# The third channel mix's down product by two levels, with its sums of quarters in fewer operations

## The chip, the cores and the metric

The kernel runs on one core of a Trainium2 chip. The metric is the device time of one execution in microseconds (us), the median of several runs. Engines are named as the profile names them: PE is the matrix engine (PEld its weight loads), DVE the vector engine, ACT the scalar engine, POOL the engine whose queue issues the weight sums' transfers here, SP the engine whose queue issues most loads.

## The reference

The input is x, 2048 tokens of 512 channels, float32. All products are in float32.

```python
n = layernorm(x)
h = layernorm(n) * ln1_g + ln1_b;  hh = h shifted by one token
k, v, r = (h*m + hh*(1-m)) @ W.T            # three mixes m, three weights 512 x 512
n = n + sigmoid(r) * wkv(k, v) @ Wo.T
h = layernorm(n) * ln2_g + ln2_b;  hh = h shifted by one token
kk = (h*cm_mk + hh*(1-cm_mk)) @ Wkey.T      # 512 -> 2048
kv = silu(kk) @ Wval.T                      # 2048 -> 512: the channel mix's down product
sr = sigmoid((h*cm_mr + hh*(1-cm_mr)) @ Wcr.T)
x = x + n + sr * kv
z = layernorm(x)
out = x + (silu(z @ Wg.T) * (z @ Wu.T)) @ Wd.T   # 512 -> 2048 -> 512
```

## The kernel before, in words

**Tiling.** The 2048 tokens are four blocks of 512. A product of 512 tokens with a 512 x 512 weight is a "unit". Tokens, inputs and outputs are halved, and most units use a fast 2 x 2 scheme with seven products instead of eight (`unit`; only six early units go plainly, `plain_unit`). Each of the seven is a product of 256 x 256 x 256: four matmuls of 128 x 128 by 256 columns. Three of the seven use sums of the weight's quarters (S1, S2, S3, S4 stand for the four sums), and operands use T1 to T4, sums of the activation's quarters. T3 is written over the quarter B12.

**Weight sums.** `prepare` is a generator for one weight: four loads of 256 KB on POOL's queue, four additions or subtractions on DVE (128 x 512 each), each followed by a store of 256 KB to scratch memory in DRAM. `prepare_all` queues them, and `prep_one` advances the first one by one operation when a credit (`credit`, raised by a fixed amount per tick) allows it. Products fetch weights through a ring of 12 tiles of 256 KB on SP's queue (`ring`).

**Parts.** The first part goes through the time mix (k, r, v and output units) and the channel mix of each block: a gate unit, four key units (`up_unit`, whose results pass through silu on ACT), and the down product (`down_unit`). Blocks overlap: the next block's mixes and norms are made on DVE and ACT while PE works on this block. The last part (`ffn_gate`, `ffn_up`, `ffn_down`) takes the four blocks one after the other.

**Down products.** In the channel mix, `down_unit` is one unit over four groups of 512 inputs: each of the seven products adds up over four groups, 28 group products of four matmuls. In the last part, `down_product` applies the scheme twice: the seven outer products (listed in `DOWN`, as A11 x B11, S4 x B22, S2 x T2, A12 x B21, S1 x T1, S3 x T3, A22 x T4, called steps here) are each split again in seven inner products, so there are 49. An inner product has four matmuls of 128 x 128 by 128 columns, one per group, and one weight load of 256 KB. Inside a step (`steps`) the inner products come in the order A11 B11, A12 B21, S2 T2, S4 B22, S1 T1, S3 T3, A22 T4; the last two are held back (`held`) and put between the first products of the next step. `quarter_sums` makes the inner sums (T1, T2, T4, T3 of quarters) of a step's operand on DVE in four operations of 128 x 512; it is asked for after the last inner product of the step two before. The sums lie in two sets of four tiles, used in turn (`room["sets"]`); seven of these eight tiles are one of the three large operand tiles (`op_tile`), taken when the last part begins. `summed` adds a step's result r into the outer results and hands finished ones to `sink`.

**Order.** PE, DVE and ACT execute exactly in the order in which the program issues to them (`manual_schedule`). A planner in the program decides that order: `tick` is called once per product, adds the product's planned length to a slack, and issues DVE work as long as the slack is positive: first the `hot` list (urgent sums), else prepared weights by credit, else the `background` list (norms, mixes). If a product needs an operand whose sums are not issued yet, `run_one(True)` issues them at that point, directly ahead of the product. `need(name)` does the same for a whole background job. `later(fn, n)` postpones a function by n products. A mix (`mix`) needs a free operand tile before it starts: at most three live at a time.

Of the kernel before, what the change touches and what calls it, by code (L numbers as in the profile page):

```python
# [9 lines left out]
F32 = mybir.dt.float32  # L10
# [5 lines left out]
P = 128  # L16
# [16 lines left out]
WK, WV, WR, WO, WCR = range(5)  # L33

TURNED = 2
PLAIN = {(0, WK), (0, WR), (0, WV), (0, WO), (1, WK), (1, WR)}
# [25 lines left out]
def rwkv_ffn_kernel(  # L62
# [4 lines left out]
    vecs: bass.AP,  # L67
    w: bass.AP,
    wd: bass.AP,
    out: bass.AP,  # L70
# [11 lines left out]
    up = ctx.enter_context(tc.tile_pool(name="up", bufs=6))  # L82
    small = ctx.enter_context(tc.tile_pool(name="small", bufs=3))
    ps = ctx.enter_context(tc.tile_pool(name="ps", bufs=6, space=bass.MemoryType.PSUM))
    pv = ctx.enter_context(tc.tile_pool(name="pv", bufs=1, space=bass.MemoryType.PSUM))
# [5 lines left out]
    htp = mixes.enter_context(tc.tile_pool(name="htp", bufs=2))  # L91
    prep = mixes.enter_context(tc.tile_pool(name="prep", bufs=6))
    pools = {"q": mixes.enter_context(tc.tile_pool(name="qp", bufs=30))}

# [27 lines left out]
    for n in range(NW):  # L122
        sources[n], sums[n] = parts(n), scratch(f"sum{n}", 4)
    for k in range(4):
        sources["d", k] = [wd[q, k] for q in range(4)]
        sums["d", k] = scratch(f"d{k}", 4)
    for q in (A11, A12, A22, S1, S2, S3, S4):
        sources["dd", q] = [wd[q, k] if q < 4 else sums["d", k][q - 4] for k in range(4)]
        sums["dd", q] = scratch(f"dd{q}", 4)

# [15 lines left out]
    def prepare(n, own):  # L146

        raw = []
        for k in range(4):
            t = prep.tile([P, 2, HB], F32, tag="raw", name="raw") if own else q_tile("q")  # L150
            paced(nc.gpsimd.dma_start(flat(t), sources[n][k]))
            raw.append(t)
        yield 1
        a11, a12, a22, a21 = raw
        for k, o, i0, i1, op in (
            (0, a22, a21, a22, ALU.add),
            (2, a21, a11, a21, ALU.subtract),
            (1, a11, a22, a11, ALU.subtract),
            (3, a12, a12, a11, ALU.subtract),
        ):  # L160
            tt(o, i0, i1, op)
            nc.gpsimd.dma_start(sums[n][k], flat(o))
            yield

    def ring(src):
        t = wring.tile([P, 2, HB], F32, tag="w", name="w")
        nc.sync.dma_start(flat(t), src)
        return t
# [6 lines left out]

    def down_weight(q, k):

        if k >= 4:
            need_sums(("dd", q))
            src = sums["dd", q][k - 4]  # L180
        elif q >= 4:
            need_sums(("d", k))
            src = sums["d", k][q - 4]
        else:
            src = wd[q, k]
        return ring(src).rearrange("p a (h c) -> p (a h) c", c=P)
# [62 lines left out]
    credit = [0.0, 0.0]  # L249

    def prep_one():
        item = preps[0]
        if item[1] > 0:
            return False
        try:
            if next(item[2]) is not None:
                item[1] = WAIT
        except StopIteration:
            preps.popleft()
            finished.add(("sums", item[0]))  # L260
            if len(preps) > 1 and item[3] > 1:
                begin(preps[1])
            elif preps:
                begin(preps[0])
        return True

# [6 lines left out]
    def prepare_all(ns, own, depth):  # L273
        empty = not preps
        for n in ns:
            preps.append([n, 0, prepare(n, own), depth, False])
        if empty:
            for item in list(preps)[:depth]:
                begin(item)
# [731 lines left out]
    def up_unit(b, g):  # L1011
# [3 lines left out]
        def sink(i, j, c):  # L1015
            t = q_tile("s")
            nc.scalar.activation(t, c, AF.Silu)
            s[i, j] = B[(B11, B12, B21, B22)[2 * i + j]] = t

# [11 lines left out]
    def down_unit(b):  # L1031
# [8 lines left out]

        unit([WVAL + g for g in range(4)], [Lazy((b, g)) for g in range(4)], sink, True, done)

# [53 lines left out]
    def ffn_up(b, g):  # L1096
        s = gated.pop((b, g))
        hid = hidden.setdefault(b, {})

        def sink(i, j, c):  # L1100
            q = (B11, B12, B21, B22)[2 * i + j]
            if q not in hid:
                hid[q] = hidden_tile()
            tt(hid[q][:, g], c, s[i, j], ALU.mult)
            if g == 3:
                made.add((b, q))
                if q in (B11, B22):
                    quarter_sums(b, 0 if q == B11 else 1)

        def done():  # L1110
            if g == 0:
                for t in (T1, T2, T4):
                    hid[t] = hidden_tile()
            urgent((b, "f", g), sums_of({t: hid[t][:, g] for t in hid}))
            if g == 3:
                made.update((b, t) for t in (T1, T2, T4, "T3"))

# [4 lines left out]

    hidden, made, asked = {}, set(), set()
    room = {}
# [5 lines left out]
    def last_room():  # L1130

        room["hidden"] = ctx.enter_context(tc.tile_pool(name="hidden", bufs=7))
        pools["q"] = ctx.enter_context(tc.tile_pool(name="fq", bufs=15))
        more = ctx.enter_context(tc.tile_pool(name="more", bufs=1))
        m, _ = op_tile("quads")
        tiles = [m[:, k] for k in range(7)]
        tiles.append(more.tile([P, 2, HB], F32, name="quad"))
        tiles = [t.rearrange("p a (h c) -> p (a h) c", c=P) for t in tiles]
        room["sets"] = tiles[:4], tiles[4:]

    def quarters(t):
        return {2 * k + m: t[:, :, k, m * P : (m + 1) * P] for k in range(2) for m in range(2)}

    def quarter_operand(b, n):

        x = quarters(hidden[b][DOWN[n][1]])
        new = room["sets"][n % 2]
        x[T1], x[T2], x[T4] = new[:3]
        x["T3"] = new[3] if n < 2 else x[B12]
        return x  # L1150

    def quarter_sums(b, n):
        x = quarter_operand(b, n)
        asked.add((b, n))

        def run():
            for o, i0, i1 in (T1, B12, B11), (T2, B22, T1), (T4, B21, T2), ("T3", B22, B12):
                tt(x[o], x[i0], x[i1], ALU.subtract)
                yield

        urgent((b, "quarters", n), run())

    def down_product(b, sink, final):
        base = {}

        def summed(n, r):
# [26 lines left out]
            else:  # L1193
                add("u2", "u2")
                sink(1, 0, base["u2"])

        def steps(n):
# [3 lines left out]
            st = {}  # L1201
            x = quarter_operand(b, n)

            def product(dst, q, k, first):
                if k in (T1, T2, T4, "T3"):
                    while (b, n) not in asked:
                        flush_one()
                    while (b, "quarters", n) not in finished:
                        run_one(True)
                wt = down_weight(a, q)  # L1210
                for g in range(4):
                    mm = nc.tensor.matmul(  # L1212
                        dst,
                        lhsT=x[k][:, g, :],
                        rhs=wt[:, g, :],
# [41 lines left out]
            def seventh():  # L1257
# [9 lines left out]
                if n + 2 < 7:  # L1267
                    quarter_sums(b, n + 2)
                summed(n, r)

# [3 lines left out]
        for n in range(7):  # L1274
            t = DOWN[n][1]
            while (b, t if t != T3 else "T3") not in made:
                flush_one()
            one = steps(n)
# [21 lines left out]
    def ffn_down(b):  # L1300
# [18 lines left out]

        down_product(b, sink, final)  # L1320

    early = [WV, WCR, WO] + [WKEY + g for g in range(4)] + [WVAL, WVAL + 1]
    late = [n + g for g in range(4) for n in (WG, WU)] + [("dd", A11)]
    late += [("d", k) for k in range(4)] + [("dd", q) for q in (S4, S2, A12, S1, S3, A22)]

# [27 lines left out]
    for b in range(NB):  # L1355
# [6 lines left out]
        if b + 1 < NB:  # L1362
            out_unit(b + 1)
        need((b, "ck"))
        if nxt:
            push(f"norm{b + 2}", time_norm(b + 2))
        for g in range(4):
            up_unit(b, g)
            if b == 1 and g == 0:
                credit[1] = 0.55  # L1370
            if g == 0:
# [11 lines left out]
        if b == NB - 1:  # L1383
            push((0, "z", "t"), ffn_in(0), op_free)
        down_unit(b)
        if nxt:
            for n, u in (("k", k_unit), ("r", r_unit), ("v", v_unit)):
                u(b + 2)
    while preps:
        need_sums(preps[-1][0])  # L1390
    need((0, "z"))
    ffn_gate(0, 0)
    mixes.close()
    last_room()
    for b in range(NB):
        for g in range(4):
# [16 lines left out]
def _layout(inputs):  # L1413
# [32 lines left out]
    )  # L1446
    def quarter_quarter(i, j, m, k):
        at = slice(i * HB + m * P, i * HB + (m + 1) * P)
        lo = j * HB + k * P

        q = [down[at, g * H + lo : g * H + lo + P].T for g in range(4)]
        return np.stack(q, axis=1).reshape(P, 4 * P)

    places = ((0, 0), (0, 1), (1, 1), (1, 0))
    wd = np.stack(
        [np.stack([quarter_quarter(i, j, m, k) for m, k in places]) for i, j in places]
    )
# [3 lines left out]
        "vecs": np.ascontiguousarray(vecs),  # L1461
        "w": np.ascontiguousarray(w),
        "wd": np.ascontiguousarray(wd),
    }
# [19 lines left out]
```

## Time and profile before

| | |
|---|---|
| Median of 3 runs | 1238.17 us (1238.16 to 1238.85) |
| Profiled execution | 1239.38 us, of it the span from first to last instruction 1237.6 us |
| PE busy | 1228.9 us, 99% of the span |
| PE's weight loads | 1101.8 us, 89% |
| DVE busy | 711.9 us, 58% |
| ACT busy | 358.0 us, 29% |
| POOL busy | 153.1 us, 12% |
| DMA | 293.27 MB, mean 237 GB/s |
| Mean granted PE clock | 0.998 |

The third block's channel mix (blocks are counted from 0 in the code, so it is block 2) has its down product at about 506 to 562 us, overlapped at both ends with the last key unit and the fourth block's gate unit. The last part runs from about 645 us to the end; its first down product is at 770 to 818 us.

In a row of the timeline, the first figure is the start, the second the time that the merged instructions took, then engine, line, operation, output and input tiles, and the number of instructions; what stands in brackets is idle time of that engine before the row and what ended it. Each float32 matmul has two records.

### The profile page before, as it was taken

To read this page: it belongs to the slowest core of one execution; us is meant where nothing else is said; L and a number is where in the kernel's file an instruction comes from. 1 tells how busy PE (TensorE), PEld (TensorE's weight loads), DVE (VectorE), ACT (ScalarE), POOL (GpSimd) and SP (SyncE) were. 2 spreads that over 40 slices of the span, in tenths; PEclk is the share of its full clock that TensorE was granted. 3 is DMA by queue.
4 is the path that set the end of the run, shared out by engine and by line. 5 is a ranking of instruction groups with operands and counts; after the bars stand their busy time and mean duration, and the time that the engine had idled before them with its cause. 6 is when DMAs were issued, how large, how long until landed. Compare 5 with 4: busy or idle time off the path is not lost.

```text
span 1237.6 us, 18092 instructions
## 1 busy us (share of the span) xinstructions
PE 1228.9 (99%) x6524; PEld 1101.8 (89%) x6524; DVE 711.9 (58%) x1315; ACT 358.0 (29%) x663; POOL 153.1 (12%) x278
## 2 busy tenths in 40 slices
PE   8999999999999999999999999999999999999998
PEld 7888888888888888888888888998899888998898
DVE  5877686587684757533542365556546365563466
ACT  5534352252532425202311222212221222112211
POOL 1332221222212121222100000000000000000000
PEclk9999999999999999999999999999999999999999
DMA  5768995889877887898756645895459755785576
GB/s 184 255 216 281 311 314 199 307 310 316 276 245 246 291 273 241 261 319 301 248 143 191 215 144 157 270 334 154 143 182 310 271 145 149 239 300 156 153 217 209
DMA packets 139871, 293.27 MB, mean 237 GB/s; under 512 B 17528, under 2 KB 18696, under 8 KB 138504
## 3 DMA queue, kind: packets, MB, share of 16 engines
q1 hardware_dynamic: 116736, 219.20, 56.2%
q0 software_dynamic: 21440, 70.27, 15.5%
q10 hardware_dynamic: 1608, 2.65, 0.6%
q8 instruction: 53, 0.87, 0.3%
q14 instruction: 34, 0.28, 0.1%
HBM read 250.11 MB, written 41.95 MB: 236 GB/s over the span
## 4 chain that ended last, share of the span: by engine, by line
PE 96%; DVE 2%; ACT 1%; DMA 1%; issue 0%; DVEq 0%
PE ps L558 54%; PE ps L1212 14%; PE accv L558 11%; PE accx L558 11%; PE ps L660 5%; PE ps L443 1%; DVE e L395 0%; DMA w<-in_w 0%; DVE mix L395 0%; DMA x<-in_x 0%; ACT mix L873 0%; ACT hT_a L865 0%; DVE q L387 0%; ACT mix L496 0%; DVE st L401 0%; DVE resid L387 0%
## 5 line engine op out<-in xcount | busy, mean ns | idle before, releaser
L558 PE MATMUL ps<-zT,w 128*128 128x256 f32 x1280 | 289.5, 379 | 0.0
L558 PEld LDWEIGHTS ps<-zT,w 128*128 128x128 f32 x1280 | 241.9, 190 | 32.2
L558 PE MATMUL ps<-mix,w 128*128 128x256 f32 x920 | 210.7, 379 | 0.0
L558 PEld LDWEIGHTS ps<-mix,w 128*128 128x128 f32 x920 | 174.5, 190 | 23.6
L387 DVE TENSOR_TENSOR u<-u,accx 128x512 f32<-128x512 f32 x66 | 45.2, 686 | 115.5 <-ACT accx L593 115.5
L1212 PE MATMUL ps<-w,hid 128*128 128x128 f32 x832 | 104.5, 275 | 0.0
L558 PE MATMUL ps<-w,t 128*128 128x256 f32 x456 | 102.2, 379 | 0.0
L1212 PEld LDWEIGHTS ps<-w,hid 128*128 128x128 f32 x832 | 99.8, 192 | 0.8
L558 PEld LDWEIGHTS ps<-w,t 128*128 128x128 f32 x456 | 86.4, 190 | 11.7
L1212 PE MATMUL ps<-w,quads 128*128 128x128 f32 x704 | 89.0, 275 | 0.4 <-ACT r L1224 0.4
L578 ACT COPY accv<-ps 128x512 f32<-128x512 f32 x66 | 37.7, 570 | 176.5 <-PE ps L558 175.4
L1212 PEld LDWEIGHTS ps<-w,quads 128*128 128x128 f32 x704 | 84.2, 192 | 0.9 <-ACT r L1224 0.5
L593 ACT COPY accx<-ps 128x512 f32<-128x512 f32 x66 | 37.7, 571 | 153.7 <-PE ps L558 152.0
L387 DVE TENSOR_TENSOR u<-ps,u 128x512 f32<-128x512 f32 x66 | 45.6, 691 | 62.6 <-PE ps L558 62.2
L387 DVE TENSOR_TENSOR raw<-raw 128x512 f32<-128x512 f32 x92 | 63.3, 688 | 20.1 <-DMA raw<-d 10.7
L589 ACT COPY u<-ps 128x512 f32<-128x512 f32 x66 | 38.6, 585 | 122.9 <-PE ps L558 122.9
L660 PE MATMUL ps<-mix,w 128*128 128x256 f32 x320 | 72.4, 386 | 1.1 <-DVE mix L395 1.1
L1224 ACT COPY r<-ps 128x128 f32<-128x128 f32 x112 | 29.8, 266 | 142.1 <-PE ps L1212 142.1
L660 PEld LDWEIGHTS ps<-mix,w 128*128 128x128 f32 x320 | 61.4, 194 | 10.2 <-DVE mix L395 1.8
L1306 POOL DMA_DIRECT2D out<-resid x12 | 8.6, 716 | 491.5 <-DVE resid L387 491.5
L558 PE MATMUL accv<-zT,w 128*128 128x256 f32 x256 | 60.6, 379 | 0.0
L558 PE MATMUL accx<-zT,w 128*128 128x256 f32 x256 | 60.5, 379 | 0.0
(168 smaller groups left out, 1654.4 us busy)
## 6 DMA issues: line engine op xcount, KB each, us to landing
w<-sum SPq DMA_DIRECT2D x312, 256.0 KB, 3.4
w<-in_w SPq DMA_DIRECT2D x254, 256.0 KB, 3.8
w<-dd SPq DMA_DIRECT2D x112, 256.0 KB, 3.6
raw<-in_w POOLq DMA_DIRECT2D x48, 256.0 KB, 5.5
sum<-raw POOLq DMA_DIRECT2D x48, 256.0 KB, 4.2
w<-d SPq DMA_DIRECT2D x48, 256.0 KB, 3.7
q<-in_w POOLq DMA_DIRECT2D x36, 256.0 KB, 6.3
sum<-q POOLq DMA_DIRECT2D x36, 256.0 KB, 4.7
```

The costliest lines, as they stand in the source:

```text
L387: nc.vector.tensor_tensor(out, a, b, op)
L443: nc.tensor.transpose(flat[:, t * P : (t + 1) * P], h[:, t, c * P : (c + 1) * P], ident)
L558: mm = nc.tensor.matmul(pz[:, m, :], lhsT=lhsT, rhs=rhs, start=first and g == 0 and m == 0 and k == 0, stop=g == last and k == 1, skip_gro ...
L578: "z", A11, B11, True, pop_held, read=lambda: nc.scalar.copy(accv, acc["z"])
L589: nc.scalar.copy(tmp["u2"], acc["z"])
L593: nc.scalar.copy(accx, acc["z"])
L660: mm = nc.tensor.matmul(acc[i, j][:, m, :], lhsT=act[:, k, lo] if by_token else wg[:, k, lo], rhs=wg[:, k, :] if by_token else act[:, k, : ...
L1212: mm = nc.tensor.matmul(dst, lhsT=x[k][:, g, :], rhs=wt[:, g, :], start=first and g == 0, stop=g == 3, skip_group_check=True,)
L1224: nc.scalar.copy(st["r"][:, m, n * P : (n + 1) * P], st["z"])
L1306: eng.dma_start(out_t[b][:, tokens, cols], rs[b][:, tokens, cols])
```

## The change

Five things are changed.

- The third block's channel-mix down product (`b == TWO`) goes through `down_product` instead of `unit`. Its operands are the four groups' silu results, in four tiles; an operand's inner sums are made per group. T1 and T3 come from one operation of 2 x 128 columns per group (4 operations), T2 and T4 from one of 128 columns per group each (8 operations). `summed` is postponed by two products there, except in the last step, so that the next sums are asked for before the results' additions. During this product no weight sum is advanced by credit (`credit[1] = 0.0`).
- The tile for the inner sums (`set_room`) is taken at the third block, ahead of its key units, and kept to the end. T3 now always has a tile of its own.
- The weight of this product is laid out in quarters of quarters as a new input `wv`, and gets seven sets of weight sums more (`("v", "q", q)`), queued ahead of the last part's. The scratch for the sums of Wval's quarters is laid out so that a quarter of it, [128 partitions x 4 groups x 128 columns], can be read as one tile: four runs of 512 bytes per partition. Twelve ring loads and 16 of the preparation's loads read it so.
- `prep_one` goes on to the next weight at once after a weight's fourth operation. The credit from the second block on is 0.66 instead of 0.55. No new weight is begun during the fourth block's down product (`halted`); the sets left are prepared during the last part, from its own pool of tiles.
- `have_operand` waits for an operand's tiles one by one, in place of the set `made`.

```diff
+        if b == TWO:
+            credit[1] = 0.0
+            down_product("v", b, sink, done)
+            credit[1] = 0.66
+        else:
+            unit([WVAL + g for g in range(4)], [Lazy((b, g)) for g in range(4)], sink, True, done)
...
+    def set_room():
         m, _ = op_tile("quads")
...
+        pairs = m.rearrange("p s a (h c) -> p s (a h) c", c=P)
+        room["pairs"] = pairs[:, 0:2], pairs[:, 4:6]
...
         def run():
-            for o, i0, i1 in (T1, B12, B11), (T2, B22, T1), (T4, B21, T2), ("T3", B22, B12):
-                tt(x[o], x[i0], x[i1], ALU.subtract)
+            x = quarter_operand(u, n)
+            order = (T1, B12, B11), (T2, B22, T1), (T4, B21, T2), ("T3", B22, B12)
+            if u[0] == "v":
+                for g in range(4):
+                    t = ops[u[1], g][DOWN[n][1]]
+                    tt(
+                        room["pairs"][n % 2][:, :, g, :],
+                        t[:, :, P:],
+                        t[:, 0, :].rearrange("p (m c) -> p m c", m=2),
+                        ALU.subtract,
+                    )
                 yield
+                order = order[1:3]
+            for o, i0, i1 in order:
+                for xg in x:
+                    tt(xg[o], xg[i0], xg[i1], ALU.subtract)
+                yield
...
                 if n + 2 < 7:
-                    quarter_sums(b, n + 2)
-                summed(n, r)
+                    quarter_sums(u, n + 2)
+                if f == "v" and n < 6:
+                    later(lambda: summed(n, r), 2)
+                else:
+                    summed(n, r)
...
     early = [WV, WCR, WO] + [WKEY + g for g in range(4)] + [WVAL, WVAL + 1]
-    late = [n + g for g in range(4) for n in (WG, WU)] + [("dd", A11)]
-    late += [("d", k) for k in range(4)] + [("dd", q) for q in (S4, S2, A12, S1, S3, A22)]
+    late = [("v", "q", q) for q in (A11, S4, S2, A12, S1, S3, A22)]
+    late += [n + g for g in range(4) for n in (WG, WU)] + [("d", k) for k in range(4)]
+    late += [("d", "q", q) for q in (A11, S4, S2, A12, S1, S3, A22)]
...
         need((b, "ck"))
+        if b == TWO:
+            set_room()
```

## The prediction

> **What bounds the kernel now.** I read the page first, its engine shares and its chain that ended last.
>
> ```profile
> PE 1228.9 (99%) x6524; PEld 1101.8 (89%) x6524; DVE 711.9 (58%) x1315; ACT 358.0 (29%) x663; POOL 153.1 (12%) x278
> PE 96%; DVE 2%; ACT 1%; DMA 1%; issue 0%; DVEq 0%
> ```
>
> The matrix engine is the bound over the whole span. A change gains what it takes out of PE's stream, minus every wait that it opens there. Next, busy time by windows: the stretch before the third channel mix's down product, the stretch that holds it, and a down product by two levels of the last part.
>
> ```profile
> 480.00:506.00 26.00, 26.00 (x130) 22.99 (x129) 18.44 (x29) 15.20 (x25) 4.31 (x8) 1.00 0.79 253
> 506.00:562.00 56.00, 56.00 (x261) 49.31 (x260) 19.54 (x31) 5.28 (x9) 12.89 (x24) 1.00 0.87 292
> 770.00:818.00 48.00, 48.00 (x406) 47.28 (x405) 29.88 (x55) 8.78 (x30) 2.06 (x3) 1.00 0.86 278
> ```
>
> PE is never idle there. After stretch and length, a row has the busy time of PE, PEld, DVE, ACT and POOL, the granted clock, the DMA share and GB/s. DVE works 19.5 of 56 us beside the down product as it is. Then PE's timeline, for the pace of the two kinds of product; each matmul is two records.
>
> ```profile
> 504.65 1.89 PE L558 MATMUL ps<-w,s 128*128 128x256 f32 x8
> 506.37 1.89 PE L558 MATMUL accx<-mix,w 128*128 128x256 f32 x8
> ...
> 779.35 1.06 PE L1212 MATMUL ps<-w,quads 128*128 128x128 f32 x8
> 780.24 1.06 PE L1212 MATMUL ps<-w,hid 128*128 128x128 f32 x8
> 782.92 1.95 PE L1212 MATMUL ps<-w,quads 128*128 128x128 f32 x16
> 784.02 0.29 DVE L387 TENSOR_TENSOR r<-ps,r 128x128 f32<-128x128 f32 x1 [2.45 <-PE ps L1212]
> 784.22 0.68 DVE L387 TENSOR_TENSOR quads<-hid 128x512 f32<-128x512 f32 x1
> ```
>
> From start to start, four matmuls of 256 columns take 1.727 us (mean over the longer runs), four of 128 take 0.893. The second product in the row at 782.92 starts at 783.81: DVE begins 0.21 us after a product's end, and its next operation, which reads none of its result, 0.20 us after a 0.29 us one.
>
> **What PE gains.** The third block's down product goes from 4 groups x 7 = 28 products of 1.727 us, 48.36 us, to 49 of 0.893, 43.76 us: 4.60 us less. PE's stream is otherwise of the same length.
>
> **What DVE gets in that stretch.** Each of the seven steps adds 4 differences of 2 x 128 columns (0.425 us, the 128x256 addition into r), 8 of 128 (0.29), and the inner additions 0.29 + 0.425 + 0.29: 1.70 + 2.32 + 1.0 = 5.0 us, 35.1 in all. Seven combining additions of 0.69 add 4.8, the eight results' operations stay, 5.5; two of 0.69 go. That is about 45 us by durations in 43.8 us of PE; started back to back, operations overlap by some 0.09 us each (0.20 us from start to start for 0.29), which leaves a few us of slack. So what counts is which operation stands ahead of which. The built order of the changed kernel shows three places where PE's next product needs an operation issued just ahead of it. In the kernel before, this happens only in the first block.
>
> Place A, sixth step (S3 x T3). The T2 quarters stand behind the addition into r of the fifth step's last product, and PE's very next product needs them. From that product's end: 0.21 to the addition, 0.20 to the first difference, 0.29 for it, about 0.1 to PE: its first matmul starts 0.80 us late, and the other differences follow at 0.20, inside PE's own 0.22. With durations laid end to end (0.21 + 0.29 + 0.29 + 0.1, and 0.07 more before each of three matmuls) it is 1.1. I take 0.8, the overlapped rows.
>
> Place B, seventh step (A22 x T4). Here the whole set of sums stands behind the addition: four 0.425 us operations (1.34 at an estimated 0.335 from start to start) come before the same four. 0.21 + 0.20 + 1.34 + 0.29 + 0.1 = 2.14; end to end 2.8. I take 2.2, just above the overlapped figure, as its 0.335 is not a row.
>
> Place C, the fourth block's key mix. In the trace of before, it is built between 487 and 492 us, 70 us ahead of use. After, the tile "quads" holds one of three operand tiles from the third block on, and urgent sums hold back background work; the built order puts the mix's first multiplication behind the last result's operations, one product before the first key product. From the end of the down product's last product: 0.21, then 0.40, 0.73 and 0.73 for three operations each reading the last, 0.61, and 0.75 for the mix's first chunk, 0.1 to PE: 3.53 us, where 1.73 is due: 1.8. The nearest row for PE's side is the first block, where the same wait is seen:
>
> ```profile
> 107.17 1.41 DVE L395 SCALAR_TENSOR_TENSOR mix<-hT_b,vec,mix 128x512 f32<-128x512 f32 x2
> 107.99 0.30 PEld L558 LDWEIGHTS ps<-w,mix 128*128 128x128 f32 x2 [0.78 <-PE ps L558]
> 108.02 2.18 PE L558 MATMUL ps<-w,mix 128*128 128x256 f32 x8 [0.41 <-PE ps L558]
> 108.63 1.16 PEld L558 LDWEIGHTS ps<-w,mix 128*128 128x128 f32 x6 [0.35 <-DVE mix L395]
> ```
>
> PE starts about 0.1 us after the first chunk and pauses again for the second; that product takes 2.01 us to the next where 1.73 is usual, 0.28 more. Place C: 2.1, between 1.9 and 2.4. Queued behind the mix on DVE are its own sums and a weight sum; the key unit's fourth product (T2) needs the second of them, by the same walk 1.3 us after it is ready.
>
> The other steps' sums have 5 to 6 us of products ahead of them in the same order and end 1 us or more early: nothing, since the products before them cover 4.0 us of DVE work; without that cover each is a second place B. One product near 432 us needs an operation that now lands within 0.1 us of its time: 0 to 0.5, taken as 0.
>
> **What is moved.** Seven weight sums more (28 loads and 28 stores of 256 KB on POOL's queue, 28 x 0.688 = 19.3 us of DVE) lie beside PE, since DVE is busy 58%. Five of the last part's sets move to 660 to 742 us, and their first use comes at 766. Cost nothing; a set asked for too early would cost its 2.75 us and its load's 5.5 us to landing. In the down stretch no set is begun. DVE's in-order waits for such loads exist before as well, up to 9.8 us at 574, without a pause of PE. On SP's queue the ring's loads come one per 0.893 us, as in the last part (86% DMA share, no wait), and the residual's store and loads keep their place, more than 12 products ahead of a use. The last part's own reordering changes no product's lead in the built order: nothing.
>
> Twelve weights of the stretch (three in each S step) are read in pieces of 512 bytes, four times the packets. No load in the trace has that shape; the nearest rows are queue q1 while the last small stores ran (1232 to 1238 us) and in a down product (778 to 817):
>
> ```profile
> q1 hardware_dynamic: 702, 0.52, 26.0%
> q1 hardware_dynamic: 5969, 10.87, 85.5%
> ```
>
> Share x 16 engines x window / packets: 35.6 ns at 741 bytes, 89.4 ns at 1821 bytes, 48 and 49 ns per KB. By bytes such a load costs the same as another, and at 35.6 ns a packet an S step needs 4 x 0.715 + 3 x 1.14 = 6.3 us against 6.25 of PE: nothing. The far bound is 89.4 ns for each, whatever its size; see the last rival.
>
> **Sum.** -4.60 + 0.8 + 2.2 + 2.1 = +0.5 us; with all waits at their ends +0.1 to +1.7. On the profiled execution (1239.38, span 1237.6) that is 1239.9. Its own time lies 1.21 above the median of the runs, 1238.17, which I forecast: 1238.7. Measurement tells about 0.2%, 2.5 us, from no change.
>
> **Does the clock fall in these waits?** The trace has one place with pauses this size, at the start:
>
> ```profile
> 9.00:10.00 1.00, 0.70 (x7) 0.46 (x5) 0.90 (x4) 0.88 (x2) 0.00 (x0) 1.00 1.04 369
> 10.00:11.00 1.00, 0.24 (x1) 0.24 (x2) 0.48 (x1) 0.97 (x3) 0.95 (x1) 1.00 1.05 389
> 11.00:12.00 1.00, 1.00 (x4) 0.76 (x4) 0.90 (x3) 0.97 (x3) 0.07 (x1) 0.52 1.04 389
> 12.00:13.00 1.00, 1.00 (x4) 0.82 (x3) 0.89 (x3) 0.97 (x3) 0.00 (x0) 0.50 1.06 393
> 13.00:14.00 1.00, 1.00 (x4) 0.82 (x3) 0.48 (x1) 0.17 (x1) 0.00 (x0) 0.50 0.53 197
> 14.00:15.00 1.00, 1.00 (x5) 0.81 (x5) 0.00 (x0) 0.00 (x0) 0.00 (x0) 0.78 0.00 0
> ```
>
> After pauses of about 1 us each, the granted clock (third figure from the right) stands at a half for some 3.4 us: 0.48 + 0.50 + 0.50 + 0.22 = 1.7 us lost. The page "TensorE: Matmul & The Clock Gate" of the Trainium skill ("Why this matters for your kernels") speaks against this change too, but sets the limit at idle gaps over about 3 us. By its rule no wait here, 2.2 us at most, costs clock and the sum stays 1238.7.
>
> By the row, two falls of 1.7 us make it 1242.1. After the 0.41 us wait at 107 us the clock stays 1.00, and much of PE's work before 11 us is sparse transposes, so I keep the sum and leave the fall to the range.
>
> **The rivals.** Faster: DVE hides its sums as it does in the last part, where the same 49 products lose nothing. For it: those rows. Against: there four operations of 0.69 us stand in time ahead of their product. With A and B free and C at most its 2.1: 1233.6 to 1235.7. Chance 0.08. Slower, by the clock: a pause of about half of a 3.4 us stretch decides, as at 8 to 11 us, and B and C are the places. One fall, 1.7 us, gives 1240.4, still within 0.2%; two give 1242.1. Chance of over 0.2% this way 0.18. Slower, by the pieces of 512 bytes: from about 73 ns a packet, two S steps in a row use up the ring's lead (12 x 0.893 less 3.6 us to landing, 7.1). At 89.4 ns an S step needs 11.4 us for 6.25; the pairs S4, S2 and S1, S3 cost 3.3 and 9.1, about 1250. Against: 35.6 ns at 741 bytes. Chance 0.06. A weight sum that lands late ahead of place A, or the wait at 432, adds 0.06.
>
> **How the numbers follow.** No change 0.62, faster 0.08, slower 0.18 + 0.06 + 0.06 = 0.30. The range runs from a little above the faster case, 1235.9, to two falls of the clock, 1242.3; outside are most of the faster case and the pieces' case.
>
> **What would show it.** Right: 49 products of 0.893 us with no pause up to the sixth step, then idle PE released by DVE before the quarters' products of the sixth and seventh steps (about 0.8 and 2.1 us) and about 1.8 us before the first key product of the fourth block; granted clock 1.00. Wrong: PE busy throughout the stretch (faster), half clock behind place B or C, or waits of the ring's loads in the S steps (slower).

## The result, and the profile after

The changed kernel takes 1251.86 us in the median of five runs (1249.26 to 1253.21), the kernel before 1238.34 beside it: a ratio of 1.0106 (95% interval 1.0091 to 1.0121). It is slower by 13.5 us, and the forecast of 1238.7 with its range up to 1242.3 was wrong. The profiled execution has 1251.86, span 1250.1 us.

The page first: its engine shares, then the chain that ended last, by engine.

```profile
PE 1231.8 (99%) x6692; PEld 1107.9 (89%) x6692; DVE 756.5 (61%) x1453; ACT 363.1 (29%) x688; POOL 186.9 (15%) x334
...
PE 86%; DMA 5%; DVE 4%; issue 2%; ACT 1%; POOL 1%; DVEq 0%; POOLq 0%; ACTq 0%
```

PE is still 99% busy, but now only 86% of the chain is PE's, 96% before, and 5% is DMA. These shares don't price the loss: e5_both of the experiments, which is faster than the kernel before, has 85% and 5%. PE's busy time rose although its stream is 4.6 us shorter: a matmul at half clock counts as busy, and e10_both_wait1, which runs as many matmuls with no fall of the clock, has 1224.2 us. PE's timeline has five rows that begin with an idle time of over half a microsecond and that the kernel before has not:

```profile
266.74 6.76 PE L595 MATMUL ps<-mix,w 128*128 128x256 f32 x16 [3.79 <-ACT u L626]
...
333.02 8.86 PE L595 MATMUL ps<-mix,w 128*128 128x256 f32 x32 [2.32 <-ACT u L626]
...
549.95 1.16 PE L1306 MATMUL ps<-w,quads 128*128 128x128 f32 x8 [0.58 <-DVE quads L424]
...
558.39 1.16 PE L1306 MATMUL ps<-w,quads 128*128 128x128 f32 x8 [1.92 <-DVE quads L424]
...
573.27 2.23 PE L595 MATMUL ps<-mix,w 128*128 128x256 f32 x8 [1.51 <-DVE mix L432]
```

The last three are the forecast's places A, B and C. The first two lie some 180 and 240 us ahead of the changed product: the one at 267 in the third block's time mix (its v unit), the one at 333 in a key unit of the second block's channel mix. Windows behind the waits at 267, 333 and 558 us show the clock (third figure from the right, a mean over the window):

```profile
266.00:273.00 7.00, 6.26 (x15) 4.95 (x16) 6.65 (x11) 1.76 (x4) 0.38 (x1) 0.51 0.71 213
334.00:338.00 4.00, 4.00 (x12) 3.24 (x11) 3.28 (x6) 1.87 (x3) 1.63 (x3) 0.57 0.88 250
559.00:564.00 5.00, 5.00 (x27) 4.81 (x27) 4.14 (x11) 0.53 (x2) 0.00 (x0) 0.66 0.61 147
```

In the first, PE works for 6.26 us at half clock and loses 3.1. In the others 4.00 x 0.43 and 5.00 x 0.34 are 1.7 us each. After the 1.51 us wait at 573 the clock stays 1.00.

Who holds PE at 266.74? The chain of waits, followed back from there (start, length, what):

```profile
247.17 9.08 DMA raw<-val
...
257.62 0.70 DVE raw L424
...
261.35 0.63 DVE r L428 x2
...
266.22 0.48 ACT u L626
...
266.74 3.35 PE ps L595 x7
```

A load for a weight sum (`raw<-val`, one of the new sets, read in pieces of 512 bytes) lands 9 us after issue. The subtraction that needs it stands next in DVE's order, and DVE stands still for 5.84 us:

```profile
257.62 1.42 DVE L424 TENSOR_TENSOR raw<-raw 128x512 f32<-128x512 f32 x2 [5.84 <-issue]
```

("issue" says that this view names no releaser; the chain names the load.) Behind it wait operations of the third block's own work (`r`), behind these ACT, and in ACT's order stands `u`, the copy that releases PE's next product. At 333 us the same happens with the set loaded at 314 to 318 us. No ring load in pieces holds PE anywhere.

### The profile page after: what moved, and what is told of

Read it like the earlier page. It is cut to its first block, busy times and chain, and to the rows that moved or that the text cites. A ratio compares the mean times of both kernels' runs of the same rounds, so it can differ in the third digit from the quotient of the medians.

```text
span 1250.1 us, 18791 instructions
## 1 busy us (share of the span) xinstructions
PE 1231.8 (99%) x6692; PEld 1107.9 (89%) x6692; DVE 756.5 (61%) x1453; ACT 363.1 (29%) x688; POOL 186.9 (15%) x334
## 4 chain that ended last, share of the span: by engine, by line
PE 86%; DMA 5%; DVE 4%; issue 2%; ACT 1%; POOL 1%; DVEq 0%; POOLq 0%; ACTq 0%
PE ps L595 45%; PE ps L1306 17%; PE accx L595 9%; PE accv L595 9%; PE ps L697 4%; DMA raw<-val 2%; PE ps L480 1%; DMA raw<-in_w 1%; DMA q<-d 1%; DVE raw L424 1%; DMA vq<-raw 1%; DVE e L432 0%; ACT mix L533 0%; DVE q L424 0%; DVE mix L432 0%
## 5 line engine op out<-in xcount | busy, mean ns | idle before, releaser
L595 PE MATMUL ps<-mix,w 128*128 128x256 f32 x920 | 216.3, 386 | 7.6 <-ACT u L626 6.1
L1306 PE MATMUL ps<-w,quads 128*128 128x128 f32 x1000 | 130.9, 276 | 2.9 <-DVE quads L424 2.5
L1306 PEld LDWEIGHTS ps<-w,quads 128*128 128x128 f32 x1000 | 122.4, 193 | 4.1 <-DVE quads L424 2.9
L424 DVE TENSOR_TENSOR raw<-raw 128x512 f32<-128x512 f32 x100 | 68.8, 688 | 50.2 <-DMA raw<-in_wd 16.2
L1318 ACT COPY r<-ps 128x128 f32<-128x128 f32 x140 | 37.2, 266 | 178.7 <-PE ps L1306 178.7
L1306 PE MATMUL ps<-w,hid 128*128 128x128 f32 x672 | 88.7, 275 | 0.0
L1306 PEld LDWEIGHTS ps<-w,hid 128*128 128x128 f32 x672 | 82.7, 192 | 0.6
L595 PE MATMUL ps<-w,t 128*128 128x256 f32 x360 | 80.6, 379 | 0.0
L595 PEld LDWEIGHTS ps<-w,t 128*128 128x128 f32 x360 | 68.4, 190 | 9.3
L697 PE MATMUL ps<-mix,w 128*128 128x256 f32 x320 | 70.8, 380 | 1.1 <-DVE mix L432 1.1
L424 DVE TENSOR_TENSOR r<-ps,r 128x256 f32<-128x256 f32 x69 | 24.8, 359 | 63.1 <-PE ps L1306 59.5
```

What stands on the lines that cost most here:

```text
L424: nc.vector.tensor_tensor(out, a, b, op)
L595: mm = nc.tensor.matmul(pz[:, m, :], lhsT=lhsT, rhs=rhs, start=first and g == 0 and m == 0 and k == 0, stop=g == last and k == 1, skip_gro ...
L697: mm = nc.tensor.matmul(acc[i, j][:, m, :], lhsT=act[:, k, lo] if by_token else wg[:, k, lo], rhs=wg[:, k, :] if by_token else act[:, k, : ...
L1306: mm = nc.tensor.matmul(dst, lhsT=x[g][k] if f == "v" else x[0][k][:, g, :], rhs=wt[:, g, :], start=first and g == 0, stop=g == 3, skip_gr ...
L1318: nc.scalar.copy(st["r"][:, m, n * P : (n + 1) * P], st["z"])
```

## The experiments

**1. The loads' shape, and where the two halves of the loss lie.** Four kernels. The first takes the pieces out of the preparation's loads by reading other data.

```diff
-            sources[f, "q", q] = [fine[f, q, k] for k in range(4)]
+            src = q % 4 if f == "v" else q
+            sources[f, "q", q] = [fine[f, src, k] for k in range(4)]
```

> Edit: the 16 preparation loads that read the scratch of Wval's sums in four runs of 512 bytes per partition read a quarter of the input wv in one run of 2 KB instead (so the S weights' inner sums are made of plain quarters; everything else, the order on every engine too, is as in the changed kernel). Theory 1, late landing: in the changed kernel's profile these loads land 7.0 to 9.6 us after issue at 245 and 314 us, where loads of 2 KB runs take about 5; DVE stands in order at the first subtraction, ACT's copy of u comes late, and PE waits 3.79 us at 267 and 2.32 us at 333, each followed by a half-clock stretch (3.4 and 1.7 us). Then the two waits go: 1251.9 - 11.2 = 1240.7 us (1239.5 to 1242), no idle PE between 120 and 540 us. Theory 2, the number and the density of the sets (seven more, credit 0.66), whatever their shape: the waits stay, 1249 to 1253 us.

Measured: 1244.5 us (1244.27 to 1246.11), between the two theories and nearer to the first. The wait at 267 us falls to 1.09, that at 333 to 0.37 us. Together with 0.6 to 0.9 us at 220 and 727 us something is left that the shape doesn't explain.

The second keeps the data and turns the scratch's layout round.

```diff
-        dram.tile([4, P, 2 * HB], ...).rearrange("g p (k m c) -> g p k m c", k=2, m=2)
+        dram.tile([4, P, 2 * HB], ...)
...
-        sums[WVAL + g] = [v[g].rearrange("p k m c -> p (k m c)") for v in vals]
+        sums[WVAL + g] = [
+            v[:, :, g * P : (g + 1) * P].rearrange("j p c -> p j c") for v in vals
+        ]
...
-            fine["v", 4 + q, k] = vals[q][:, :, kk, m, :].rearrange("g p c -> p g c")
+            fine["v", 4 + q, k] = vals[q][2 * kk + m]
```

> Edit: the scratch of Wval's sums is laid out the other way round, so that the quarters of quarters are read in one run of 2 KB (16 preparation loads, 12 ring loads), and the 16 stores and 48 ordinary ring loads of these sums go in four runs of 512 bytes. The order on every engine is that of the changed kernel. Theory 1, late landing of the preparation's loads: the waits at 267 and 333 us go, 1240.7 us (1239.5 to 1242); the ring's loads in pieces are 12 deep ahead and cost nothing, as in the stretch of 515 to 545 us. Theory 2, the sets' number and density: 1249 to 1253 us. If loads in pieces cost wherever they stand: a new wait of PE for a ring load in the channel mixes' ordinary down products, above 1242 us.

Measured: 1241.37 us (1239.58 to 1242.93). There is no wait at 267 us, 0.69 and 0.30 at 326 and 331, and 1.17 at 220. The 48 ring loads that now come in pieces cost PE nothing that shows. (Four of a unit's seven products use weight sums, S1 to S4, not three as the kernel's description has it; with four groups and three blocks that makes 48.)

The third leaves the loads alone and moves the sums of a step.

```diff
             one = steps(n)
+            while f == "v" and (u, n) in asked and (u, n) not in finished:
+                run_one(True)
             one[0]()
```

> Edit: in the third block's down product, the sums for a step are issued to DVE ahead of the step's first product, so in front of the additions of the step before; in the resulting order the fourth block's key mix also starts earlier, well ahead of its first use. Theory: the waits before the sixth and seventh steps (0.58 and 1.92 us idle), the half-clock stretch after the latter (1.7 us) and the one before the first key product of the fourth block (1.51 us idle) go, and nothing new comes: 1251.9 - 0.75 - 3.8 - 1.8 = 1245.5 us (1244 to 1247). Rival, DVE has no more time in this stretch and the wait only moves to the results' additions or to the next step: 1249 to 1253 us. The waits at 267 and 333 us stay in both.

Measured: 1245.43 us (1242.84 to 1246.38), as expected. PE shows no pause from 340 to 700 us; the waits at 267 and 332 are there (3.70 and 2.13). So A, B and C together with the clock were worth about 6.4 us, and DVE has the time.

The fourth uses the one-level product again (`if b == TWO:` made `if False:`), and prepares the sets for nothing.

> Edit: the third block's down product goes through the one-level unit as before the change; the seven sets of weight sums for the two-level product are still prepared, but used by nothing. The order up to that product is the changed kernel's. Theory 1, the preparation's loads in pieces of 512 bytes make the early waits, and the two-level product itself has no part in them: 1251.9 - 6.3 (its three waits with the clock) + 4.6 (PE's shorter stream) = 1250.2 us (1248 to 1252), waits at 267 and 333 us present. Rival, the early waits are a chance of one execution or belong to the two-level product: 1238 to 1240 us.

Measured: 1246.45 us (1245.95 to 1247.3), under the expected range, with waits of 3.23 and 2.02 us at 267 and 331. About 8 us come from preparing the seven sets and from what else of the change is left in this kernel (the credit, the jump to the next weight, the early tile); the two-level product has no part in them. That it is 3.8 us less than expected is mostly the clock, which falls once here for 1.7 us (0.97 of full speed over 240 to 300 us) and not at 333 us, where the changed kernel loses 3.1 and 1.7 us.

**2. Pieces alone, or more than pieces?** The kernel before with 16 of its own loads in pieces:

```diff
+            if own and n in late[:4]:
+                piece = w[n, :, :, k // 2, (k % 2) * P : (k % 2 + 1) * P]
+                dst = flat(t).rearrange("p (g c) -> p g c", g=4)
+                paced(nc.gpsimd.dma_start(dst, piece.rearrange("g p c -> p g c")))
```

> Edit: the kernel before, with the 16 loads of its first four sets of late weight sums (issued at about 230 to 287 us) made in four runs of 512 bytes per partition instead of one of 2 KB (pieces of the four quarters are mixed, so those sums hold other numbers; nothing else changes). Theory, pieces alone make the landing late: the loads land at 7 us or more instead of 5.4 in the median, DVE stands longer at the first subtractions, and PE waits somewhere between 235 and 300 us: 1240.5 to 1245 us. Rival, it takes the changed kernel's closer sets as well (a set every 16 us instead of 18 to 19, and the next set's loads issued at once): landing later by 2 us or less, no idle PE, 1238.5 us.

Measured: 1238.44 us (ratio 0.9997, 0.9988 to 1.0006): no change. The 16 loads land at 5.9 us in the median where the same ones take 5.4, and POOL issues one in 0.75 instead of 0.54 us; one wait of 1.26 us at 319 us is seen, and the start is 1.8 us faster in this profile. Pieces by themselves are not the 9.6 us.

**3. What holds the loads back.** POOL's queue in the changed kernel around them:

```profile
237.87 0.54 POOL L193 DMA_DIRECT2D vq<-raw  x1 [0.66 <-DVE raw L424]
245.06 1.56 POOL L182 DMA_DIRECT2D raw<-val  x2 [6.65 <-issue]
246.62 0.56 POOL L193 DMA_DIRECT2D vq<-raw  x1
247.17 1.48 POOL L182 DMA_DIRECT2D raw<-val  x2
```

The product that the first load is paced by ends at about 242.4; in e5_both, below, the load is issued then. Here POOL goes on standing for 2.6 us and issues at 245.06. In between, at 244.91, SP issues the store of the first block's residual, 1 MB (`res<-x`). From 247 to 248 us that store's large packets (49 of together 0.40 MB) take 104.3% of the 16 DMA engines' time, and POOL's software queue has none; most of the set's loads move from 250 to 255 us.

POOL's pause is in the kernel before too, where nothing depends on it:

```profile
262.54 1.61 POOL L151 DMA_DIRECT2D raw<-in_w  x3 [2.50 <-issue]
```

By count it stands there ahead of the queue's 114th transfer, and in e1_contig too (2.55 us). In the changed kernel it comes ahead of the 112th, the first in pieces, and in e8_before_pieces after 104 whole transfers and 2 in pieces. All four fit if a load in four pieces counts as four of 113. For stores in pieces the count doesn't come out: in e2_layout POOL stands 2.98 us ahead of a store at 183.12 whose data DVE has ready 2.2 us earlier, after 72 whole transfers and 11 such stores, which would be 116. Two kernels test what the pause does. One puts five more transfers ahead of everything:

```diff
+            if split[0]:
+                split[0] -= 1
+                for at in (slice(0, HB), slice(HB, 2 * HB)):
+                    paced(nc.gpsimd.dma_start(flat(t)[:, at], sources[n][k][:, at]))
```

> Edit: the first five loads of weight sums (at 20 to 40 us) are made in two halves of 1 KB per partition, so that POOL's queue has five transfers more ahead of everything; the order on PE, DVE and ACT is the changed kernel's, pieces of 512 bytes included. Theory, a pause in POOL's queue: in the kernel before and in e1_contig POOL stands 2.5 us, for nothing that the profile shows, ahead of its 114th transfer, in e8_before_pieces where each load in pieces counts as four ahead of the 114th again, and in the changed kernel at the first load in pieces after 111 transfers (four do not fit in the two that are left). That puts this set's loads at 245 to 248 us, behind the residual's store of 1 MB issued at 244.9 us. Five transfers more move the pause ahead of a store at about 236 us: the loads are issued from 242.4 us, land by 252 us, PE's wait at 267 us falls from 3.8 to under 1 us with no half clock, the one at 333 us stays at about 2 us: 1251.9 - 6.5 = 1245.4 us (1244 to 1247.5). Rival, the pieces alone: a wait of 3 to 4 us at 267, 1249 to 1253 us.

Measured: 1246.55 us (1245.2 to 1248.35). The pause has moved to the stores, and the loads in pieces start on time:

```profile
237.96 1.63 POOL L200 DMA_DIRECT2D vq<-raw  x3 [10.60 <-DVE raw L431]
241.95 1.53 POOL L189 DMA_DIRECT2D raw<-val  x2 [2.37 <-PE ps L602]
```

and though one of them lands only after 9.2 us, PE's wait at 263 to 267 us is 0.69 without a fall of the clock. The later one is 2.86. The other kernel leaves the pause where it is and moves the 1 MB store:

```diff
-            nc.sync.dma_start(resid[b], x1s.pop(b))
+            x1 = x1s.pop(b)
+            stores.append([5, lambda: paced(nc.sync.dma_start(resid[b], x1))])
```

> Edit: the residual's store of 1 MB per block is issued five products later on SP's queue (for the first block at about 253 instead of 244.9 us); nothing else moves in the order. Theory, the 1 MB store stands in front of the loads: POOL's first load in pieces is still issued at about 245 us, but the loads of this set land 5.5 to 7 us after issue instead of 7.0 to 9.6, and PE's wait at 267 us falls from 3.8 to about 1 us: 1246 us (1244.5 to 1248). Rival, the pieces or the pause alone set the landing: wait of 3 to 4 us, 1249 to 1253 us.

Measured: 1244.03 us (1242.78 to 1245.53), and no wait at 267 at all. The four loads are issued as late as before, 244.7 to 247.5, but land earlier:

```profile
DMA to landing us min/median/max: 7.0/8.5/9.6
```

is the changed kernel's line for these four loads, and e9_store's is

```profile
DMA to landing us min/median/max: 3.6/5.2/5.7
```

So the wait at 267 us needs both: the pause that puts the loads behind the store, and the store. Either one taken away, it goes (but for 0.69 us in e7_shift), with the pieces still there. Experiment 1 has to be read again with this. In e2_layout a pause of that size stands at 183 us, as said, and none ahead of this set, whose loads are issued on time:

```profile
243.84 0.54 POOL L182 DMA_DIRECT2D raw<-val  x1 [4.11 <-PE ps L595]
```

They land in up to 8.5 us all the same, and PE doesn't wait. So the wait at 267 is gone there together with the pause; that the longer runs took it away is not shown. In e1_contig two of the four loads are issued ahead of the pause, and 1.09 us are left.

The wait at 333 us is another matter: it is 2.0 to 2.9 us in all five kernels with the pieces and this distance from load to subtraction, and 0.4 to 1.3 in the three with 2 KB runs (e1_contig, e2_layout, e5_both). There the shape counts, for some 1.5 us, but not by the time to landing: at most 8.9 us in the changed kernel and 8.9 in e2_layout. What differs is the issue. The changed kernel's four loads start over 3.8 us (313.7 to 317.5), e2_layout's over 2.3 (307.9 to 310.2): POOL takes 0.75 instead of 0.54 us for each, and waits 1.53 instead of 0.64 us for a store to land ahead of the last two. No run takes these two apart.

**4. Distance from the load to the subtraction.** `WAIT` becomes `WAIT + 3` for the seven new sets.

> Edit: the changed kernel with its loads in pieces of 512 bytes, but 8 instead of 5 products (13.8 instead of 8.6 us of PE) between the end of a set's loads and its first subtraction on DVE, for the seven new sets alone. In the resulting order the wait ahead of the sixth step is gone too; those ahead of the seventh step and of the fourth block's key mix stay. Theory, DVE stands in order behind loads that land up to 9.6 us after issue: the loads land as late as before, but PE's idle time at about 267 and 333 us goes: 1251.9 - 11.2 - 0.75 = 1239.9 us (1238.5 to 1242.5). Rival, the loads in pieces slow PE's own loads or the stores, not DVE's order: the waits stay, 1247 to 1252 us.

Measured: 1242.76 us (1241.9 to 1243.21). The wait at 267 goes, though the loads of the set at 268 us land in up to 8.9 us. For the set behind that wait the test is weaker: its loads are issued at 248.1 to 251.0 us here and land in 6.8 at most, not as late as before. At 319 and 326 us 1.01 and 1.12 are left, the fourth block's mix waits 2.08 us instead of 1.51, and there are waits of 0.64 and 0.72 us at 724 and 743. The mechanism holds; the gain was 2.9 us smaller than expected, and these short waits are the likely reason: the later sets lie elsewhere in DVE's order and meet other needs.

**5. Put together.** First both repairs, e2_layout's and e3_ab's.

> Edits of e2_layout (the preparation reads Wval's sums in 2 KB runs) and e3_ab (a step's sums issued ahead of its first product) together. Theory: the two act in different places and add up: e2_layout's 1241.4 less the waits of 0.75, 2.1 and 1.8 us that e3_ab took away = 1236.7 us (1235.5 to 1238), about 1.9 us under the kernel before; what is left of the expected 4.6 us gain is lost to short waits at 220, 326, 331 and 444 us that e2_layout still shows. Rival, the early and late waits share a cause (DVE has no more time), so that one edit only moves the other's wait: 1240 to 1243 us.

Measured: 1235.89 us (1234.62 to 1237.43), ratio 0.9978 (0.9969 to 0.9987). They add up. What is left of idle PE between 110 and 700 us is 1.26 and 0.31 us at 325 and 331. Then the same without the jump to the next weight:

```diff
-        if item[5] == 4 and item[3] == 1:
-            return prep_one()
```

> Edits of e5_both, and prep_one no longer goes on to the next weight at once after a weight's fourth operation (the kernel before's manner). The sets then stand 15 to 21 us apart instead of 16, the seven sets end at 349 instead of 328 us. Theory, the closer sets cause what is left of the waits (220, 326, 331 and 444 us, 2.7 us in e2_layout): 1236.7 - 2.7 = 1234.0 us (1233 to 1235.5). Rival, these short waits come from the place of a subtraction in DVE's order, whatever the distance of the sets: other short waits, 1235.5 to 1238 us.

Measured: 1257.68 us, far from both. With the sets further apart the last ones are made late, and the last part waits for them, up to

```profile
829.78 2.05 PE L1303 MATMUL ps<-w,quads 128*128 128x128 f32 x8 [8.80 <-DMA w<-dq]
```

A part of the change that looked like detail carries the seven sets: without it they cost 22 us at the other end. Last, e5_both with one product more between load and subtraction of the seven sets:

> Edits of e5_both (2 KB runs for the preparation, a step's sums ahead of its first product), and 6 instead of 5 products between the loads of the seven new sets and their first subtraction. e5_both still waits 1.26 us at 325 and 0.31 us at 331 us for DVE behind these loads. Theory: the distance takes them away, 1235.9 - 1.6 = 1234.3 us (1233.5 to 1235.5), 4 us under the kernel before. Rival, the moved subtractions meet another product's needs, as the short waits did in e6_wait at 319 and 326 us: 1235.5 to 1238 us.

Measured: 1234.71 us (1234.42 to 1234.86) against 1239.04, ratio 0.9965 (0.9953 to 0.9978). It is faster than both kernels, and its runs lie within 0.5 us, where the changed kernel's spread over 4. Its row at the place of the second wait:

```profile
324.18 7.17 PE L595 MATMUL ps<-mix,w 128*128 128x256 f32 x32 [0.42 <-ACT u L626]
```

## Why the prediction was wrong

Against e10_both_wait1, which issues the same matmuls, the profiled changed kernel is 17.0 us longer (1250.1 to 1233.1): 10.5 by the two-level product's first matmul (511.0 to 500.5), 4.7 inside it (first to last matmul 58.7 to 54.0), and 1.8 behind it. The last two figures are the forecast's subject; the first is the one that it left out.

**What PE gains: right.** The forecast's pace gives 53.9 us from the stretch's first two-level matmul to its last, with the other products between them; e10_both_wait1 takes 54.0.

**Places A, B, C: right in place and in size.** The idle times in brackets are 0.58, 1.92 and 1.51 us, but they count from the modelled end of the product before. From start to start, as the forecast counted, A's first product comes 0.74 us late and the next 0.11 more, B's 2.09 and 0.11; C's comes 1.7 late and takes 2.06 us to the next where 1.73 is usual. That is 0.85, 2.2 and 2.0; taken were 0.8, 2.2 and 2.1.

**Pieces of 512 bytes in the ring: right.** No wait of PE for a ring load in the stretch.

**What is moved: here it failed.** "Seven weight sums more ... lie beside PE, since DVE is busy 58%. ... Cost nothing". The term put at nothing measured 11.4 us: from start to start, PE's stream is 7.1 us late by the wait at 267 us and the clock's fall there, and 4.3 by those at 333. DVE's average is no cover: the subtraction stands in its order at a place where the load may not have landed, and what stands behind it is PE's next operand. The forecast had read DVE waiting 9.8 us at 574 without harm and took this for a rule; there no product of PE came to wait for what stood behind it. It also had a price of 5.5 us for landing from the kernel before. Issued on time, as in e5_both (242.4 to 244.8 us), the set's loads have 6.9 to 9.2 us until DVE comes to the subtraction at 251.7. In the changed kernel POOL's pause leaves them 3.9 to 6.7, and they take 7.0 to 9.6. Nor was 5.5 us the price at every place: the set at 314 us took up to 8.9. The forecast gave "a weight sum that lands late" a chance of 0.06, and looked for it ahead of place A.

**The clock: the rival was right, the sum was not.** The fall was left to the range. It came after B, and after the two early waits, 6.5 us in this execution. The kernel before loses 1.7 us at its start in its own profile, after pauses of 0.90 and 1.06 us; the changed kernel, which has only the one of 1.06 us there, loses none: its product after the 0.41 us wait that both kernels have starts at 106.44 instead of 108.02, 1.6 us earlier.

What stays open: from start to start, with the clock, the terms are -4.6 for PE's stream, 7.1 and 4.3 for the early waits, 4.7 inside the stretch (A, B and the fall behind B), 2.0 for C and -1.6 at the start: 11.9 us of the 12.5 between the two spans. The other 0.6 was not placed.

## What to carry to other kernels

Before extra work is called free because its engine has time, find in the issued order what stands behind its first wait for a transfer, and compare the distance with the worst landing, not the median one. A large store on another queue belongs in that comparison. The layout is worth a look too: the 48 ring loads that run far ahead took pieces of 512 bytes without a wait of PE, while the preparation's loads, with little distance, lost some 1.5 us at one place by them.

## What the runs showed of the hardware

**A pause in POOL's queue.** In the kernel before and in e1_contig POOL stands 2.50 and 2.55 us ahead of its 114th transfer with nothing shown that it waits for. With a load in pieces of 512 bytes counted as four, the pause's place fits in the changed kernel and in e8_before_pieces as well; e2_layout's stores in pieces don't fit that count exactly. What POOL does in the pause isn't seen; e7_shift shows that five transfers more move it.

**The clock's fall is not decided by the pause's length alone.** The changed kernel and seven of the experiments (e1, e2, e3, e4, e6, e7, e9) have four pauses of 2.86 to 3.79 us, and all came with a fall; of eleven pauses of 1.92 to 2.50 us four did, and of place B's 1.92 us three in six, while e9_store's 2.50 us had none. The page "TensorE: Matmul & The Clock Gate" of the Trainium skill (section "What's actually happening" of its Part 1) tells of a free-running window of about 3.4 us. The runs agree with that: the half-clock stretches of the changed kernel are 3.4, 3.4 and, at 267 us, 6.8 us long by windows of 1 us, and two of them begin 1.3 us after the pause's end. They don't agree with its condition of a whole idle window there, as 1.92 us was enough in three kernels.
